# A mixture-of-experts stage on one core: large and small experts in turns, the last tiles of two experts side by side, and written orders for POOL and VectorE

## The chip, the core and the metric

One core of a Trainium2 chip runs the whole program in one launch. The metric is the device time of that launch in microseconds (us). TensorE (PE) multiplies matrices, VectorE (DVE) and ScalarE (ACT) work elementwise, GpSimd (POOL) here mainly issues indirect DMAs (gathers and scatters by a table of row numbers), and SyncE (SP) issues plain DMAs.

## The reference

A graph layer over 12500 nodes of 256 features, and behind it a mixture of 64 experts:

```
h  = feats * rsqrt(deg_out)
m  = segment_sum(h[src], dst) * rsqrt(deg_in)          # 212500 edges
x  = m @ W_gc + b_gc + feats @ W_res + b_res
vals, idx = top_k(x @ Wg + bg, 2); gates = softmax(vals)
for each expert e and each node n that chose it (at most 1024 of them):
    y[n] += gate * (gelu(x[n] @ w1[e] + b1[e]) @ w2[e] + b2[e])   # 256 -> 512 -> 256
z  = batchnorm(x + y) ;  out = layernorm(feats + z)
```

All is float32. A node has two experts, so its row of the sum is added to twice.

## The kernel before

The program has four stages one after another: degrees (to about 580 us), edge sums with the dense layer and the routing (to about 2550 us), the experts (about 2550 to 3430 us), and the two normalizations. The change touches only the experts.

Before the expert stage the kernel has x with the two gates of each node in DRAM (`x2_d`, 258 columns), the running sum in DRAM (`z_d`, which holds x), and tables that give for every expert, by slot, the row to gather and the row to add to. Experts are ranked by how many tokens they have; `TOKENS` (in units of 16) is a fixed bound for each rank, and a path for the case that it does not hold follows the stage and is skipped here. Rank i's tokens are cut into *parts* of at most four *tiles* of 128 tokens; the last tile of a rank holds what is left, 16 to 112 tokens, or is full. There are 83 parts and 241 tiles. `parts` lists them: the last rank first, then the ranks from the largest to the smallest.

For each part q the loop in the program does this:

- `begin` (L1727), called three parts ahead: on a new expert it reads the expert's number into registers of SP and VectorE (one load for up to four experts), has VectorE copy that expert's table columns (`sort_slots`), has SP load the weights (`load`, one DMA of 1026 KB and one for the bias, pool `w` with three buffers), and has POOL gather the part's rows (`gather`, L1638; pool `xg` with 16 tiles).
- `hidden` (L1667, L1671): for each of four blocks of 128 hidden units two matmuls over the part's tokens, then ScalarE's gelu into `h1`.
- `turned` (for part q + 1): VectorE computes that part's gates (`gates_of`, L1682), TensorE transposes its tiles (L1653) into the one PSUM tile `xtp`, VectorE copies it to `xT` (L1658).
- `outputs` (L1694 to L1701): for each tile four matmuls with the tokens as stationary columns and w2 as moving data into `yp` (two PSUM buffers), VectorE adds the bias (L1699) and multiplies by the gate (L1700) into `yo` (six buffers), and POOL scatters with addition into `z_d`. Scatters of one expert need not wait for each other, since no node has an expert twice; scatters of different experts do.

The order of TensorE in this stage is the program's order (`manual_schedule` for PE): hidden of q, transposes of q + 1, outputs of q. The orders of VectorE, POOL, SP and ScalarE are made by a scheduler when the program is built. [...]

## Time and profile before

| What | Value |
|---|---|
| three runs | 3574.12, 3606.88, 3612.92 us; median 3606.88 |
| the profiled execution | 3578.72 us, span 3576.8 us, mean granted TensorE clock 0.829 |
| PE busy | 2531.0 us (71%) |
| POOL busy | 2175.5 us (61%) |
| DVE busy | 1800.6 us (50%) |
| ACT busy | 798.8 us (22%) |
| expert stage, first transposes to last scatter | about 2560 to 3433 us |

The profile shows the execution on its own clock, from the first instruction of the program to the last. Shares of busy time are means over stages with different limits, so a change in one stage is read from windows inside it. Matmuls are pipelined and their ends are modelled; the difference between two starts is the better measure of what one costs. POOL's gathers and scatters appear as DMA_INDIRECT: the time is POOL's own, for issuing; the data lands later.

### The profile page before, as it was taken

What the parts mean: (1) busy time and instruction counts of PE and PEld (TensorE: products, weight loads), DVE (VectorE), ACT (ScalarE), POOL (GpSimd) and SP (SyncE); (2) the same over time, 40 slices, a digit from 0 to 9 for tenths busy, and PEclk for the clock granted to TensorE, in tenths of its full rate; (3) what the DMA queues carried; (4) which work ended last, traced back from release to release, by engine and by line L of the source; (5) the groups of instructions that cost most, each with busy time, mean ns of one, the idle gap of its engine ahead of it and who ended that gap; (6) DMA issues with size and microseconds to landing.
All of it is one profiled execution on the core that took longest, in us unless ns stands there. A gap on an engine that the chain in (4) does not pass through costs nothing. (4 is left out here: it accounts for less than half of the span.)

```text
span 3576.8 us, 40049 instructions
## 1 busy us (share of the span) xinstructions
PE 2531.0 (71%) x11797; PEld 1893.4 (53%) x11797; DVE 1800.6 (50%) x7368; ACT 798.8 (22%) x1975; POOL 2175.5 (61%) x2095
## 2 busy tenths in 40 slices
PE   2526075566776667676766666677699999999966
PEld 2415043455555555554555444454377876677856
DVE  3729454355555465655555435467543333333358
ACT  2416301122111122212221111111111221122246
POOL 7250776666666666666666666665367777777610
PEclk6657566778887878897878777788899999999988
DMA  8450853444554555555544444444555666676764
GB/s 259 128 189 6 309 203 95 158 145 144 143 150 146 141 147 168 146 147 157 155 144 122 142 117 122 119 135 124 159 115 122 134 135 146 155 177 173 197 196 144
DMA packets 313919, 538.03 MB, mean 150 GB/s; under 512 B 47274, under 2 KB 233102, under 8 KB 305502
## 3 DMA queue, kind: packets, MB, share of 16 engines
q0 software_dynamic: 119360, 266.30, 28.9%
q1 hardware_dynamic: 180795, 256.19, 23.0%
q10 hardware_dynamic: 13539, 12.90, 1.2%
q8 instruction: 97, 1.59, 0.2%
q14 instruction: 128, 1.05, 0.1%
HBM read 431.02 MB, written 105.28 MB: 150 GB/s over the span
## 5 line engine op out<-in xcount | busy, mean ns | idle before, releaser
L938 POOL DMA_INDIRECT ring<-h_d,src_col x1416 | 1372.4, 969 | 711.8 <-issue 387.2
L952 PE MATMUL p<-ring,o 128*128 128x258 f32 x2832 | 902.0, 450 | 213.2 <-issue 89.7
L952 PEld LDWEIGHTS p<-ring,o 128*128 128x128 f32 x2832 | 600.4, 224 | 389.2 <-issue 214.9
L930 DVE TENSOR_SCALAR o<-lane,rel 128x128 f32<-128x128 f32 x1416 | 356.1, 297 | 402.7 <-remote 160.3
L1701 POOL DMA_INDIRECT z_d<-yo,tables x241 | 375.0, 1556 | 129.8 <-issue 58.0
L1694 PE MATMUL yp<-w,h 128*128 128x256 f32 (+7 forms) x1928 | 436.3, 381 | 0.8 <-DVE tables L1762 0.8
L1667 PE MATMUL hp<-xT,w 128*128 128x384 f32 (+22 forms) x1328 | 392.3, 449 | 9.4 <-issue 9.4
L1694 PEld LDWEIGHTS yp<-w,h 128*128 128x128 f32 (+7 forms) x1928 | 336.8, 179 | 71.0 <-issue 7.6
L1638 POOL DMA_INDIRECT xg<-x_d,tables x241 | 234.3, 972 | 183.7 <-PE xtp L1653 88.2
L1671 ACT ACTIVATE h<-hp,w 128x384 f32<-128x384 f32 (+21 forms) x332 | 178.7, 539 | 682.0 <-PE hp L1667 673.1
L1667 PEld LDWEIGHTS hp<-xT,w 128*128 128x128 f32 x1328 | 248.0, 192 | 134.1 <-issue 61.0
L1506 ACT ACTIVATE again<-again,factor 128x256 f32<-128x256 f32 x180 | 82.4, 501 | 670.3 <-issue 363.2
L986 ACT COPY s<-p 128x258 f32<-128x258 f32 x118 | 43.8, 371 | 814.8 <-PE p L952 450.0
L1658 DVE COPY xT<-xtp 128x672 f32<-128x672 f32 (+21 forms) x83 | 70.8, 853 | 305.6 <-PE xtp L1653 297.2
L1699 DVE TENSOR_TENSOR yo<-yp,bb 128x256 f32<-128x256 f32 (+7 forms) x241 | 102.0, 423 | 224.1 <-PE yp L1694 154.2
L285 POOL DMA_INDIRECT early<-in_x,src_col x130 | 135.0, 1038 | 102.4 <-DMA early_d<-early 56.3
L567 PE MATMUL deg<-o_hi,o_lo 128*128 128x98 bf16 x1254 | 107.3, 254 | 122.8 <-issue 83.8
L1481 PE MATMUL q<-r_out,tables 128*128 128x98 f32 x360 | 66.8, 315 | 150.4 <-DVE tables L1489 55.9
L1027 PE MATMUL q<-ident,s 128*128 128x128 f32 x236 | 58.9, 337 | 158.0 <-DVE tables L1489 67.5
L222 DVE TENSOR_TENSOR o_hi<-lane_b,hi 128x2450 bf16<-128x2450 bf16 (+1 forms) x67 | 95.1, 1419 | 145.8 <-remote 106.2
L565 ACT ACTIVATE s_lo<-lane_b,nb 128x128 bf16<-128x128 bf16 x396 | 121.8, 388 | 192.9 <-remote 126.7
L567 PEld LDWEIGHTS <-o_lo 128*128 128x128 bf16 x1254 | 87.5, 125 | 140.1 <-issue 91.2
(367 smaller groups left out, 3503.5 us busy)
## 6 DMA issues: line engine op xcount, KB each, us to landing
w<-in_wpack SPq DMA_DIRECT2D x64, 1026.0 KB
again<-early_d SPq DMA_DIRECT2D x90, 256.0 KB
ring<-h_d,src_col POOLq DMA_INDIRECT x1416
early_d<-early SPq DMA_DIRECT2D x65, 256.0 KB
tables<-h_d SPq DMA_DIRECT2D x104, 128.0 KB
acc<-acc_d SPq DMA_DIRECT2D x14, 896.0 KB
acc<-in_x SPq DMA_DIRECT2D x12, 1024.0 KB
x_d<-y SPq DMA_DIRECT2D x47, 258.0 KB
```

What stands on the lines that cost most here:

```text
L285: GP.indirect_dma_start(out=t[:, c % 2], out_offset=None, in_=x, in_offset=bass.IndirectOffsetOnAxis(ap=src_col[:, MC + c : MC + c + 1], a ...
L565: S.activation(s_lo[:, i], lane_b, AF.Sign, bias=nb[:, k - k0, i : i + 1])
L567: T.matmul(deg, o_lo[:, i], o_hi[:, i], start=c + i == 0, stop=False)
L930: o_last[u] = V.tensor_scalar(o_of[u][:, j], lane, rel[:, c : c + 1], None, op0=ALU.is_equal)
L938: i = GP.indirect_dma_start(out=r[:, k, :D], out_offset=None, in_=h_d, in_offset=bass.IndirectOffsetOnAxis(ap=src_col[:, c : c + 1], axis=0),)
L952: i = T.matmul(p_of[g], o_of[v][:, n], r[:, k], start=j == 0, stop=j == GR - 1)
L1638: GP.indirect_dma_start(out=g[:r], out_offset=None, in_=x2_d, in_offset=bass.IndirectOffsetOnAxis(ap=at[:r, 0, k : k + 1], axis=0),)
L1667: T.matmul(hp[:, :m], w1[:, c, j * P : (j + 1) * P], xT[:, c, :m], start=c == 0, stop=c == 1,)
L1671: S.activation(h1[:, j, :m], hp[:, :m], AF.Gelu, bias=w[:, 2 * H + 4 * D + j : 2 * H + 4 * D + j + 1],)
L1694: T.matmul(yp[:r], h1[:, j, k * P : k * P + r], w2[:, j], start=j == 0, stop=j == 3,)
L1699: V.tensor_add(yo[:r], yp[:r], bb[:r])
L1701: st = GP.indirect_dma_start(out=z_d, out_offset=bass.IndirectOffsetOnAxis(ap=at[:r, 1, k : k + 1], axis=0), in_=yo[:r], in_offset=None, c ...
```

## The change

- **Order of the experts.** Ranks are joined into pairs (`PAIR_OF`) by how many blocks of 32 the last tile of each fills: two and two, one and three, or one and one. With the token table there are 17 pairs: five of tails of 48 or 64 tokens each, twelve of a tail of 80 or 96 beside one of 16 or 32. A pair's members follow each other, the second with its parts in reverse, so that the two tails are computed in neighbouring parts. Pairs and single ranks then alternate, the largest, the smallest, the next largest, and so on. The last rank still comes first and the one before it last. As the ranks no longer follow each other, registers are loaded for one expert at a time in most cases.
- **Tails side by side.** `pair_of_outputs` gives both tails one `yp` tile: the first at row 0, the second at row 64 or 96. For each of the four hidden blocks it issues one matmul per block of 32 columns of each tail, or one of 64 for each where both tails have 33 to 64 tokens. Each half then gets its own bias, gate and scatter. All other tiles keep `outputs` as it was, with four matmuls each (`products`).
- **Gathers of at least 80 rows** (`WHOLE`): a tail of fewer tokens gathers and transposes 80 rows; hidden, copy and output still take only its tokens.
- **Orders.** VectorE joins TensorE in the program's order. POOL's gathers and scatters are chained in the program's order (`in_order`); scatters of one expert stay free among themselves. For a pair the order on POOL is: the first tail's scatter, the gathers for three parts ahead, the second tail's scatter, the second expert's other scatters. The second's scatters wait for the first's to land.
- **Gates** (`gates`) are computed just ahead of their part's outputs, behind the copy of the next part's `xT`; before, ahead of that copy and a part earlier.
- **Buffers.** Four for the weights (three before), ten for `yo` (six before).

The diff, cut to its core:

```
-        wp = stack.enter_context(tc.tile_pool(name="w", bufs=3))
+        wp = stack.enter_context(tc.tile_pool(name="w", bufs=4))
...
-        REGS = 4
+        REGS, YO = 4, 10
...
+        def in_order(i, group=None):
+            if "over" in issued:
+                return
+            if group is None or group != issued["group"]:
+                issued.update(group=group, before=issued["these"], these=[])
+            for j in issued["before"]:
+                tc.add_manual_dep(i.ins, j.ins.name, ... NoSync, SCHED_ONLY ...)
+            issued["these"].append(i)
...
-                r = min(P, m - k)
+                r = max(WHOLE, min(P, m - k))          # WHOLE = 80
...
+        def add_to_nodes(yo, at, k, group):
...
+                for before in scatters.get(mate.get(group), []):
+                    tc.add_manual_dep(st.ins, before.ins.name, ... Sync, DATA ...)
+                scatters.setdefault(group, []).append(st)
+                in_order(st, group)
...
+        def pair_of_outputs(two_of):
+            yp = ps2.tile([P, D], F32, name="yp")
+            tails = [of[5] % P for of in two_of]
+            width = SIDE if min(tails) > BLOCK and max(tails) <= SIDE else BLOCK
+            starts = [0, max(SIDE, -(-tails[0] // BLOCK) * BLOCK)]
+            for j in range(4):
+                for start, r, (w, bb, at, gate, h1, m, group) in zip(starts, tails, two_of):
+                    for k in range(0, r, width):
+                        n = min(width, r - k)
+                        products(yp[start + k : start + k + n], n, w, h1, m - r + k, j)
+            todo = []
+            for start, r, (w, bb, at, gate, h1, m, group) in zip(starts, tails, two_of):
+                part_of_yp = slice(start, start + r)
+                yo = gated(yp[part_of_yp], r, bb[part_of_yp], gate, m // P)
+                todo.append(lambda ...: add_to_nodes(yo, at, m // P, group))
+            todo[0]()
+            return todo[1]
...
-        with tc.manual_schedule(engines={mybir.EngineType.PE}):
+        with tc.manual_schedule(engines={mybir.EngineType.PE, DVE}):
...
                 h1 = hidden(given[i][0], xT, m)
-                if q + AHEAD < len(parts):
+                if q not in pair_at and q + AHEAD < len(parts):
                     begin(q + AHEAD)
                 if q + 1 < len(parts):
                     xT = turned(q + 1)
-                outputs(*given[i], table(q), gate.pop(q), h1, m, f"expert{i}")
+                mine = (*given[i], table(q), gates(q), h1, m, f"expert{i}")
+                if q in pair_at:
+                    rest = pair_of_outputs([kept.pop(pair_at[q]), mine])
+                    begin(q + AHEAD)
+                if q in pair_at or q in pair_at.values():
+                    if q not in pair_at:
+                        kept[q] = mine
+                    mine = (*mine[:5], m // P * P, mine[6])
+                if q in pair_at:
+                    rest()
+                outputs(*mine)
```

More of the change, by code (lines that the diff above doesn't have):

```diff
@@ L110, with blocks_of @@
 ]
+SIDE, BLOCK = P // 2, P // 4
+WHOLE = SIDE + 16
+def blocks_of(r):
+    return -(-r // BLOCK)
+PAIR_OF = {}
+for _k in ((2, 2), (1, 3), (1, 1)):
+    _open = []
+    for _i, _n in enumerate(TOKENS[: E - 2]):
+        _u = blocks_of(_n * TU % P)
+        if _u not in _k or _i in PAIR_OF or _i in PAIR_OF.values():
+            continue
+        _mate = [_j for _j, _v in _open if (_v, _u) in (_k, _k[::-1])]
+        if _mate:
+            PAIR_OF[_mate[0]] = _i
+            _open = [_o for _o in _open if _o[0] != _mate[0]]
+        else:
+            _open.append((_i, _u))
 RPE = CAP // P
@@ L1629, in overfull @@
             V.tensor_copy(over_n, some)
+        issued = {"group": None, "these": [], "before": []}
+        def in_order(i, group=None):
[4 more added lines that the diff above has]
+            for j in issued["before"]:
+                tc.add_manual_dep(
+                    i.ins, j.ins.name,
+                    mybir.DependencyInfo(
+                        mybir.DependencyClass.NoSync, mybir.DependencyReason.SCHED_ONLY
+                    ),
+                    reason="gathers and scatters are issued in this order",
+                )
+            issued["these"].append(i)
         def gather(at, m):
@@ L1634, in gather @@
             for k in range(0, m, P):
-                r = min(P, m - k)
+                r = max(WHOLE, min(P, m - k))
                 k //= P
                 g = two.tile([P, D2], F32, name="xg", bufs=16)
-                GP.indirect_dma_start(
+                i = GP.indirect_dma_start(
                     out=g[:r],
@@ L1643, in gather, with turn @@
                 )
+                in_order(i)
                 xg.append(g[:r])
             return xg
-        def turn(xg):
+        def turn(xg, m):
             xtp = ps1.tile([P, 2, 4 * P], F32, name="xtp")
@@ L1655, in turn @@
                     )
-            m = k * P + r
             xT = two.tile([P, 2, 4 * P], F32, name="xT")
@@ L1686, in gates_of, with products, gated, outputs @@
             return gate
-        def outputs(w, bb, at, gate, h1, m, group):
+        def products(yp, r, w, h1, a, j):
             w2 = w[:, 2 * H : 2 * H + 4 * D].rearrange("p (c d) -> p c d", d=D)
-            for k in range(-(-m // P)):
+            T.matmul(yp, h1[:, j, a : a + r], w2[:, j], start=j == 0, stop=j == 3)
+        def gated(yp, r, bb, gate, k):
+            yo = two.tile([P, D], F32, name="yo", bufs=YO)
+            V.tensor_add(yo[:r], yp, bb)
+            V.tensor_scalar_mul(yo[:r], yo[:r], gate[:r, k : k + 1])
+            return yo[:r]
+        def add_to_nodes(yo, at, k, group):
+            r = yo.shape[0]
+            st = GP.indirect_dma_start(
+                out=z_d,
+                out_offset=bass.IndirectOffsetOnAxis(ap=at[:r, 1, k : k + 1], axis=0),
+                in_=yo,
+                in_offset=None,
+                compute_op=ALU.add,
+            )
+            if group:
+                tc.declare_no_dep(st.ins, group=group, reason="no node has an expert twice")
+                tc.add_to_no_dep_group(group, st.ins)
+                for before in scatters.get(mate.get(group), []):
+                    tc.add_manual_dep(
+                        st.ins, before.ins.name,
+                        mybir.DependencyInfo(mybir.DependencyClass.Sync, mybir.DependencyReason.DATA),
+                        reason="a node can have both experts of a pair",
+                    )
+                scatters.setdefault(group, []).append(st)
+                in_order(st, group)
+        scatters = {}
+        mate = {f"expert{j}": f"expert{i}" for i, j in PAIR_OF.items()}
+        def outputs(w, bb, at, gate, h1, m, group, ks=None):
+            for k in ks or range(-(-m // P)):
                 r = min(P, m - k * P)
@@ L1693, in outputs @@
                 for j in range(4):
-                    T.matmul(
-                        yp[:r], h1[:, j, k * P : k * P + r], w2[:, j],
-                        start=j == 0, stop=j == 3,
-                    )
-                yo = two.tile([P, D], F32, name="yo", bufs=6)
-                V.tensor_add(yo[:r], yp[:r], bb[:r])
-                V.tensor_scalar_mul(yo[:r], yo[:r], gate[:r, k : k + 1])
-                st = GP.indirect_dma_start(
-                    out=z_d,
-                    out_offset=bass.IndirectOffsetOnAxis(
-                        ap=at[:r, 1, k : k + 1], axis=0
-                    ),
-                    in_=yo[:r],
-                    in_offset=None,
-                    compute_op=ALU.add,
-                )
@@ L1710, in outputs @@
-                if group:
-                    tc.declare_no_dep(st.ins, group=group, reason="no node has an expert twice")
-                    tc.add_to_no_dep_group(group, st.ins)
+                    products(yp[:r], r, w, h1, k * P, j)
+                add_to_nodes(gated(yp[:r], r, bb[:r], gate, k), at, k, group)
+        def pair_of_outputs(two_of):
[12 more added lines that the diff above has]
+                yo = gated(yp[part_of_yp], r, bb[part_of_yp], gate, m // P)
+                todo.append(lambda yo=yo, at=at, m=m, group=group: add_to_nodes(yo, at, m // P, group))
+            todo[0]()
+            return todo[1]
@@ L1715, in gnn_moe_kernel @@
+        units = []
+        for i in range(E - 2):
+            if i not in PAIR_OF.values():
+                units.append([i, PAIR_OF[i]] if i in PAIR_OF else [i])
+        units.sort(key=lambda u: -sum(TOKENS[i] for i in u))
+        order = [E - 1]
+        while units:
+            order += units.pop(0)
+            if units:
+                order += units.pop()
+        order.append(E - 2)
         parts = []
-        for i in [E - 1, *range(E - 1)]:
+        for i in order:
             n = -(-TOKENS[i] * TU // P)
@@ L1719, in gnn_moe_kernel @@
             b = 0
+            of = []
             for j in range(k):
                 m = (n - b + k - j - 1) // (k - j)
-                parts.append((i, b, min(m * P, TOKENS[i] * TU - b * P)))
+                of.append((i, b, min(m * P, TOKENS[i] * TU - b * P)))
                 b += m
+            parts += of[::-1] if i in PAIR_OF.values() else of
+        pair_at = {}
+        for q, (i, b, m) in enumerate(parts[1:], 1):
+            if PAIR_OF.get(parts[q - 1][0]) == i:
+                assert blocks_of(m % P) + blocks_of(parts[q - 1][2] % P) <= 4
+                pair_at[q] = q - 1
         AHEAD = 3
@@ L1728, in begin @@
             i, b, m = parts[q]
-            if b == 0:
-                k = 0 if i == E - 1 else i % REGS
-                if k == 0:
-                    n = 1 if i == E - 1 else min(REGS, E - 1 - i)
+            if i not in given:
+                if i not in columns_of:
+                    n = 1
+                    at = order.index(i)
+                    while n < REGS and order[at : at + n + 1] == [*range(i, i + n + 1)]:
+                        n += 1
                     _, regs = nc.values_load_multi_w_load_instructions(
@@ L1746, in begin @@
                     )
-                    given["regs"] = regs, columns
-                regs, columns = given["regs"]
-                columns_of[i] = columns[k]
+                    for k in range(n):
+                        columns_of[i + k], reg_of[i + k] = columns[k], regs[k]
                 sort_slots(i, 0)
@@ L1752, in begin @@
                     sort_slots(i, 1)
-                given[i] = load(regs[k])
+                given[i] = load(reg_of[i])
             xg[q] = gather(table(q), m)
-        columns_of = {}
+        columns_of, reg_of = {}, {}
         def sort_slots(i, which):
@@ L1770, in turned, with gates @@
         def turned(q):
+            return turn(xg[q], parts[q][2])
+        def gates(q):
             i, b, m = parts[q]
-            gate[q] = gates_of(xg[q], snd_sorted[:, i * RPE + b : i * RPE + b + 4])
-            return turn(xg.pop(q))
-        gate = {}
+            return gates_of(xg.pop(q), snd_sorted[:, i * RPE + b : i * RPE + b + 4])
+        kept = {}
         snd_sorted = one.tile([P, NSLOT], F32)
-        with tc.manual_schedule(engines={mybir.EngineType.PE}):
+        with tc.manual_schedule(engines={mybir.EngineType.PE, DVE}):
             for q in range(AHEAD):
@@ L1794, in gnn_moe_kernel @@
                     xT = turned(q + 1)
-                outputs(*given[i], table(q), gate.pop(q), h1, m, f"expert{i}")
+                mine = (*given[i], table(q), gates(q), h1, m, f"expert{i}")
[9 more added lines that the diff above has]
+                    outputs(*mine)
+                else:
+                    outputs(*mine)
                 if q == 16:
                     overfull()
+        issued["over"] = True
         with tc.If(nc.values_load(over_n[0:1, 0:1]) > 0):
@@ L1802, in gnn_moe_kernel @@
                 r = rows(a)
-                again = two.tile([P, D], F32, name="yo", bufs=6)
+                again = two.tile([P, D], F32, name="yo", bufs=YO)
                 nc.sync.dma_start(again[:r], x2_d[a * P : a * P + r, :D])
@@ L1815, in gnn_moe_kernel @@
                     gb = gates_of(g, second[:, b : b + 4])
-                    outputs(w, bb, ab, gb, hidden(w, turn(g), 4 * P), 4 * P, None)
+                    outputs(w, bb, ab, gb, hidden(w, turn(g, 4 * P), 4 * P), 4 * P, None)
     with ExitStack() as stack:
```

## The prediction

> **What bounds the kernel now.** The change touches only the expert stage, so I read that stage first by the windows view (busy time per 100 us: PE, PEld, DVE, ACT, POOL, then the granted TensorE clock, the DMA share and GB/s).

> ```profile
> 2600.00:2700.00 100.00, 100.00 (x406) 71.58 (x405) 43.58 (x175) 19.55 (x32) 70.41 (x56) 1.00 0.56 117
> ...
> 3300.00:3400.00 100.00, 100.00 (x485) 81.67 (x484) 35.73 (x96) 22.63 (x48) 63.24 (x49) 1.00 0.77 197
> sum 800.00, PE 800.00 PEld 594.98 DVE 288.79 ACT 166.87 POOL 561.84; mean PE 100.00 PEld 74.37 DVE 36.10 ACT 20.86 POOL 70.23
> ```

> TensorE is busy 800 of 800 us at clock 1.00. Nothing that shortens only another engine's work can shorten this stretch; what counts is what TensorE itself executes, and whether something new makes it wait. The groups of the stage (from 2540 to 3440 us) say what it executes:

> ```profile
> L1694 PE MATMUL yp<-w,h 128*128 128x256 f32 (+7 forms) x1928 | 436.3, 381 | 0.8 <-DVE tables L1762 0.8
> L1667 PE MATMUL hp<-xT,w 128*128 128x384 f32 (+22 forms) x1328 | 392.3, 449 | 9.4 <-issue 9.4
> L1701 POOL DMA_INDIRECT z_d<-yo,tables x241 | 375.0, 1556 | 129.8 <-issue 58.0 <-DVE yo L1700 26.5 <-DVE gate L1682 23.8
> L1638 POOL DMA_INDIRECT xg<-x_d,tables x241 | 234.3, 972 | 183.7 <-PE xtp L1653 88.2 <-DVE tables L1762 40.8 <-issue 39.0
> L1653 PE MATMUL xtp<-ident,xg 128*128 128x128 f32 (+7 forms) x482 | 65.6, 266 | 11.0 <-issue 10.5 <-DMA xg<-x_d,tables 0.5
> ```

> 241 tiles times four blocks of the hidden size are 964 matmuls on L1694; the trace has 1928, so each float32 matmul is two passes. A busy union does not price a pass, since ends are modelled; starts do. In the timeline of PE (start, length, name, count) I subtract starts:

> ```profile
> 2660.93 5.34 PE L1694 MATMUL yp<-w,h 128*128 128x256 f32 x24
> 2666.11 5.32 PE L1667 MATMUL hp<-xT,w 128*128 128x384 f32 x16
> 2671.27 0.74 PE L1653 MATMUL xtp<-ident,xg 128*128 128x128 f32 x6
> 2671.85 5.38 PE L1694 MATMUL yp<-w,h 128*128 128x256 f32 x24
> 2677.07 1.29 PE L1667 MATMUL hp<-xT,w 128*128 128x336 f32 x4
> ```

> 24 passes of full tiles take 2666.11 - 2660.93 = 5.18 us, 0.216 each; 16 hidden passes over 384 tokens take 5.16; the transposes of two full tiles and one of 80 rows 0.58, and the outputs behind these 5.22. A tile of fewer tokens costs L1694 the same eight passes. That is what the pairing attacks: 34 of the 241 tiles.

> **The change, part by part.** *Gathers of at least 80 rows.* 24 tiles have 64 tokens or fewer, and their transposes now take 80 rows. Here are a part whose last tile has 64 tokens, then one with 16:

> ```profile
> 2713.90 0.87 PE L1653 MATMUL xtp<-ident,xg 128*128 128x128 f32 x6
> 2714.70 5.45 PE L1694 MATMUL yp<-w,h 128*128 128x256 f32 x24
> 2719.98 4.47 PE L1667 MATMUL hp<-xT,w 128*128 128x320 f32 x16
> 2724.29 0.82 PE L1653 MATMUL xtp<-ident,xg 128*128 128x128 f32 x6
> 2724.94 5.49 PE L1694 MATMUL yp<-w,h 128*128 128x256 f32 x24
> 2730.36 5.43 PE L1667 MATMUL hp<-xT,w 128*128 128x384 f32 x16
> 2735.63 0.84 PE L1653 MATMUL xtp<-ident,xg 128*128 128x128 f32 x6
> ```
> ```profile
> 2756.87 0.82 PE L1653 MATMUL xtp<-ident,xg 128*128 128x128 f32 x6
> 2757.62 5.45 PE L1694 MATMUL yp<-w,h 128*128 128x256 f32 x24
> 2762.91 3.83 PE L1667 MATMUL hp<-xT,w 128*128 128x272 f32 x16
> 2766.57 0.82 PE L1653 MATMUL xtp<-ident,xg 128*128 128x128 f32 x6
> 2767.23 5.45 PE L1694 MATMUL yp<-w,h 128*128 128x256 f32 x24
> 2772.61 5.43 PE L1667 MATMUL hp<-xT,w 128*128 128x384 f32 x16
> 2777.87 0.60 PE L1653 MATMUL xtp<-ident,xg 128*128 128x128 f32 x4
> ```

> Transposes and the outputs behind them take 0.80 + 5.28 = 6.08 us with 64 tokens and 0.75 + 5.29 = 6.04 with 16, against 0.58 + 5.22 = 5.80 with 80. So 0.24 to 0.28 us is saved per tile: 24 x 0.26 = **-6.2 us**.

> *Fewer changes to narrow outputs.* An output tile of 64 tokens or fewer lengthens its run (5.42 and 5.38 against 5.18) and the hidden passes behind it (5.27 and 5.26 against 5.16): 0.35 and 0.30 us. Before, 24 tiles pay this. After, 17 pairs and the two unpaired ones of the last two experts do: 5 x 0.32 = **-1.6 us**.

> *The pairs.* By the token table 34 tails make 17 pairs: five of two tails of 48 or 64, each one block of 64 columns; twelve of a tail of 80 or 96 beside one of 16 or 32, four blocks of 32. Before, 34 x 8 x 0.216 = 58.8 us. After, a matmul per block and hidden block: 5 x 2 x 4 + 12 x 4 x 4 = 232 matmuls, 464 passes. No row of this trace shows two blocks of columns at work, so I bound it. If no passes overlap: 464 x 0.216 = 100.2 us, +41.5. If all blocks of a pair run together, a pair takes as long as one tile: 17 x 8 x 0.216 = 29.4 us, -29.4. I take a value between, from the order in which passes stand: the two passes of a matmul follow each other on the same block of columns, so the second must wait until the first has streamed, and if later passes do not overtake it, only it and the next block's first pass can run side by side. Then n matmuls take n + 1 steps: 9 for the five pairs, 17 for the twelve, 5 x 1.94 + 12 x 3.67 = 53.8 us, **-5.0 us**. The twelve four-block pairs gain nothing in this; only the five do. In the rows above every pass starts 0.216 after the one ahead, in the order of the program, which is why I lean to the ordered value.

> [...]

> *Gates and order on VectorE and POOL.* DVE is busy 36 of 100 us, and the gates move from ahead of the transposed copy to behind it. Register loads rise from 17 to 50, each some 0.34 us, hidden behind the 64% that DVE is idle:

> ```profile
> L1740 DVEq TENSOR_LOAD <-exp_row x17: 318/343/862, 2550.6 to 2617.4; - x17
> ```

> What could hurt is the copy that feeds the next hidden matmuls, since six parts now have one full output tile (1.73 us) for cover. Before:

> ```profile
> 2876.63 0.82 PE L1653 MATMUL xtp<-ident,xg 128*128 128x128 f32 x6
> 2877.29 3.62 PE L1694 MATMUL yp<-w,h 128*128 128x256 f32 x16
> 2877.49 0.96 DVE L1658 COPY xT<-xtp 128x768 f32<-128x768 f32 x1 [2.14 <-PE xtp L1653]
> L1658 DVE COPY xT<-xtp 128x896 f32<-128x896 f32 x1 | 1.1, 1091 | 5.6 <-PE xtp L1653 5.6
> ```

> The copy starts 0.20 us after the outputs. The longest behind a one-tile part has 896 elements, 1.09 us: done at 1.29 of 1.73. Nothing is added; if the cover went, six times a few tenths.

> *POOL.* The same 241 gathers and 241 scatters, in a written order. Each has about 0.30 us of its own gap:

> ```profile
> 3253.15 1.57 POOL L1701 DMA_INDIRECT z_d<-yo,tables  x1 [0.30 <-DVE yo L1699]
> 3255.02 1.43 POOL L1701 DMA_INDIRECT z_d<-yo,tables  x1 [0.30 <-issue]
> 3257.21 1.01 POOL L1638 DMA_INDIRECT xg<-x_d,tables  x1 [0.76 <-PE xtp L1653]
> 3258.53 0.91 POOL L1638 DMA_INDIRECT xg<-x_d,tables  x1 [0.30 <-PE yp L1694]
> ```

> 241 x (0.97 + 0.30) + 241 x (1.56 + 0.30) = 754 us of a stage of some 868 (2562 to 3430): 87%, the next engine behind PE. New is a wait 17 times: the second tail's scatter waits until the first has landed. Behind it on POOL stand that expert's scatters and then the next gathers; PE waits for those only if they fall three parts behind. The last scatter of the stage gives the landing time, from the chain that ended last:

> ```profile
> 3430.93 1.53 POOL z_d L1701
> 3432.79 3.70 DMA z_d<-yo,tables
> ```

> 3.7 us from its start. The changed order puts the next part's two to four gathers between (2.5 to 5.1 us, after the first scatter's own 1.86), so the wait is covered. Were it bare, 17 x 1.8 = 31 us of the 114 that POOL has free: still no bound.

> *Order of the experts, weights in four buffers, ten output buffers.* These move loads, and PE was not waiting for any. Cost nothing while PE is at 100%. At the start of the stage PE does stand still:

> ```profile
> 2579.80 8.67 PE L1667 MATMUL hp<-xT,w 128*128 128x512 f32 x16 [8.76 <-issue]
> ```

> What ends it is not shown, so I leave it in: up to 8.8 us gained, as much lost.

> **Sum.** -6.2 - 1.6 - 5.0 = -12.8 us. On the profiled execution's own 3578.7 us (span 3576.8) that is 3565.9. That execution stands with the fastest of the other runs (3574.1, 3606.9, 3612.9; median 3606.9). I lay the change on the mean of all four, 3593.2: **3580 us**. Its own range, with the start and these runs' spread, is 3555 to 3605.

> **The rivals.** *All blocks run together.* The pairs give -29.4, in all -37.2: 3556 us (3541 on the profiled run). For it: different columns, different rows of the output. Against: the two passes on the same columns stand next to each other. It also needs POOL: 868 - 37 = 831 us against 754, or 785 with every new wait bare, so it still fits. [...]

> *No overlap at all (slower).* The place is the twelve four-block pairs: 32 passes where 16 stood, 6.9 us for 3.5. +41.5 - 7.8 = +33.7: 3627 us. It decides as soon as a four-block pair takes over 4.1 us, which eats the 7.8 us of the narrow tiles. For it: every pass in the trace is 0.216 after the other. Against: they all want the same columns there.

> *The fixed VectorE order makes PE wait.* If an output in the written order waits for its buffer, the copy behind it is late. With 0.5 us at 82 parts, +41 - 12.8: 3621 us. It decides from 0.4 us of delay at six parts and 2 us elsewhere; ten output buffers speak against it.

> **How the numbers follow.** Ordered overlap 0.38, all together 0.30, none 0.20, VectorE's order 0.12. About 1% (36 us) is what a measurement of this kernel can tell from no change. The first is within it but for the runs' spread (0.06 faster, 0.02 slower); the second, 1.03%, is beyond it 7 times in 10 (0.21); the third half the time (0.10), the last three quarters (0.09). Faster 0.27, slower 0.21, the same 0.52. The range runs from the second rival on a fast run (3537) to near the third on a slow one (3640).

> **What would show it.** On the changed L1729, a pair of two tails should take 1.9 us from start to start and a four-block pair 3.7; 1.7 in both says that all blocks overlap, 3.5 and 6.9 that none do. No transpose should have fewer than 80 rows, and the 0.24 to 0.28 should be gone. PE should stay at 100.00 in every window; idle time on L1706 released by the xT copy, or POOL above 95%, would prove me wrong, and so would a clock below 1.00.

## The result and the profile after

The changed kernel takes 3580.83 us (median of 17 runs, 3563.20 to 3605.51); beside it the kernel before took 3610.55 us (17 runs). The ratio over all runs is 0.9944, 95% interval 0.9922 to 0.9966: a gain of 0.34 to 0.78%, or 12 to 28 us. The forecast of 3580 us is met, but not by its working: the pairs brought more than five times what the sum gave them, and waits of TensorE, which the sum had at nothing, took much of the surplus back. The base helped too: the sum of -12.8 us was laid on 3593.2 us, a mean of four runs, where the median of the 17 is 3610.55 and the two medians lie 29.7 us apart. That 3580 was hit is luck.

The profiled execution after has a span of 3565.6 us against 3576.8, which is 11.2 less and close to the forecast's 12.8. That too is chance. The rows of TensorE that open and close the stage (timeline: start, length, name, count, idle before and what ended it) show it, first in the kernel before, then after:

```profile
2562.07 4.50 PE L1667 MATMUL hp<-xT,w 128*128 128x176 f32 x16 [0.66 <-issue]
...
3425.03 3.76 PE L1694 MATMUL yp<-w,h 128*128 128x256 f32 x16
```
```profile
2577.93 4.16 PE L1706 MATMUL hp<-xT,w 128*128 128x176 f32 x16 [0.62 <-DVE xT L1697]
2581.93 1.04 PE L1693 MATMUL xtp<-ident,xg 128*128 128x128 f32 x8
2582.81 3.75 PE L1729 MATMUL yp<-w,h 128*128 128x256 f32 x16
2586.49 7.13 PE L1706 MATMUL hp<-xT,w 128*128 128x512 f32 x16
...
3413.43 3.76 PE L1729 MATMUL yp<-w,h 128*128 128x256 f32 x16
```

The first hidden matmul starts at 2577.93, before at 2562.07: the unchanged stages ahead took 15.9 us more in this execution. From there to the last output run the stage takes 835.5 us, before (2562.07 to 3425.03) 863.0. So the stage gained 27.5 us. The wait of 8.76 us that stood ahead of the second part's hidden matmuls is gone: 2586.49 follows the outputs directly.

The windows that answer to those of before, the groups of the stage, and what TensorE waited for:

```profile
2600.00:2700.00 100.00, 99.37 (x487) 75.56 (x486) 37.98 (x117) 21.54 (x40) 67.17 (x53) 1.00 0.61 134
...
3100.00:3200.00 100.00, 95.93 (x477) 69.40 (x476) 38.05 (x122) 19.79 (x36) 70.72 (x57) 0.98 0.71 174
...
sum 800.00, PE 786.32 PEld 593.81 DVE 307.98 ACT 170.40 POOL 576.11; mean PE 98.29 PEld 74.23 DVE 38.50 ACT 21.30 POOL 72.01
```
```profile
L1729 PE MATMUL yp<-w,h 128*128 128x256 f32 (+5 forms) x2120 | 411.7, 383 | 8.2 <-DVE yo L1733 7.9
...
L1693 PE MATMUL xtp<-ident,xg 128*128 128x128 f32 (+3 forms) x482 | 64.8, 268 | 16.1 <-issue 10.3 <-DMA xg<-x_d,tables 5.7
```

TensorE is no longer at 100 in every window: 13.7 of these 800 us are idle, and the granted clock falls to 0.98 where it was 1.00. L1729 has 192 more passes than before (2120 against 1928: 464 in place of 272 for the pairs) and yet 24.6 us less busy time. POOL rose from 70.2 to 72.0 of 100 and is far from its limit as a mean.

What a pair takes is read from the starts. First a pair of a tail of 80 or 96 with one of 16 or 32 ahead of two full tiles (32 + 16 passes), then one of two tails of 48 or 64 ahead of one full tile (16 + 8):

```profile
2618.08 5.58 PE L1729 MATMUL yp<-w,h 128*32 128x256 f32 x48
2623.50 5.32 PE L1706 MATMUL hp<-xT,w 128*128 128x384 f32 x16
...
2711.55 3.87 PE L1729 MATMUL yp<-w,h 128*64 128x256 f32 x24
2715.26 5.32 PE L1706 MATMUL hp<-xT,w 128*128 128x384 f32 x16
```

5.42 - 16 x 0.216 = 1.96 us, and 3.71 - 8 x 0.216 = 1.98 us. The forecast said 3.7 and 1.9; both at eight steps of 0.216 (1.73) is the rival in which all blocks run together, with 0.23 and 0.25 us more. Most of that lies in two starts behind the narrow passes: in the first pair the first two passes of the full tiles start 0.33 and 0.32 us behind the one ahead, the others 0.216. The single passes in the trace say the same: in the first pair four passes start within 0.02 us, the next four 0.22 us behind them, and so on, eight times four.

### The profile page after: what moved, and what is told of

Same layout as the page of the kernel before. It is cut to its first block, busy times and chain, and to the rows that moved or that the text cites. A ratio compares the mean times of both kernels' runs of the same rounds, so it can differ in the third digit from the quotient of the medians.

```text
span 3565.6 us, 40447 instructions
## 1 busy us (share of the span) xinstructions
PE 2496.3 (70%) x11920; PEld 1876.5 (53%) x11989; DVE 1799.1 (50%) x7368; ACT 798.5 (22%) x1975; POOL 2179.6 (61%) x2095
## 4 chain that ended last, share of the span: by engine, by line
PE 38%; DVE 22%; issue 11%; another core or an unknown queue 10%; POOL 3%; DMA 3%; SPq 1%; ACT 0%; DVEq 0%; ACTq 0%; POOLq 0%
PE yp L1729 11%; PE hp L1706 10%; PE p L973 8%; DVE o L951 4%; POOL ring L959 3%; PE bank L1188 2%; PE bank L1193 2%; DVE junk L1273 1%; PE xtp L1693 1%; PE tab L1326 1%; DVE y L1211 1%; PE bank L1532 1%; DVE tables L1510 1%; DMA tables<-in_src 1%
## 5 line engine op out<-in xcount | busy, mean ns | idle before, releaser
L1729 PE MATMUL yp<-w,h 128*128 128x256 f32 (+5 forms) x2120 | 411.7, 383 | 8.2 <-DVE yo L1733 7.9
L1706 PE MATMUL hp<-xT,w 128*128 128x384 f32 (+21 forms) x1328 | 388.4, 446 | 0.8 <-DVE xT L1697 0.6
L1729 PEld LDWEIGHTS yp<-w,h 128*128 128x128 f32 (+5 forms) x2120 | 320.6, 171 | 73.1 <-issue 13.5
L1706 PEld LDWEIGHTS hp<-xT,w 128*128 128x128 f32 x1328 | 248.6, 191 | 117.4 <-issue 42.1
L1697 DVE COPY xT<-xtp 128x768 f32<-128x768 f32 (+16 forms) x83 | 70.8, 854 | 333.4 <-PE xtp L1693 300.6
L1733 DVE TENSOR_TENSOR yo<-yp,bb 128x256 f32<-128x256 f32 (+6 forms) x241 | 102.2, 424 | 174.7 <-PE yp L1729 141.3
L1502 PEld LDWEIGHTS q<-r_out,tables 128*128 128x128 f32 x360 | 62.6, 230 | 176.2 <-issue 74.4
```

The costliest lines, as they stand in the source:

```text
L1502: T.matmul(p_r[:, i], wide[:, i * P : (i + 1) * P], r_out, start=True, stop=True)
L1706: T.matmul(hp[:, :m], w1[:, c, j * P : (j + 1) * P], xT[:, c, :m], start=c == 0, stop=c == 1,)
L1729: T.matmul(yp, h1[:, j, a : a + r], w2[:, j], start=j == 0, stop=j == 3)
```

## The experiments

All runs below were made on three other chips, each against the kernel before on its own chip (medians of 3153 to 3154 us): serial, two_block, blocks_outer and ahead4 on one, after_again, before_again, free_pool and before_80 on the second, the rest on the third. The stages ahead take some 430 us less there (the first hidden matmul starts at 2144.30 us in after_again, at 2577.93 in after), so the expert stage is compared: from the start of the first hidden matmul to the start of the last output pass, read from the trace. TensorE's *own work* is the stage less its idle time in it and less what half clock costs the rest (half of each stretch in which the trace has the granted clock at 0.50). It is 853.3 us in both profiles of the kernel before, and in before_ahead4 on a third chip.

| Kernel | ratio to before, 95% | stage us | idle us | own work us |
|---|---|---|---|---|
| before, first profile | | 866.3 | 9.6 | 853.3 |
| after, first profile | 0.9944 (0.9922 to 0.9966) | 838.9 | 13.7 | 820.4 |
| before_again | one run | 863.3 | 6.1 | 853.3 |
| after_again | 0.9910 (0.9894 to 0.9927) | 838.8 | 11.8 | 819.1 |
| serial | 0.9948 (0.9931 to 0.9964) | 847.3 | 0.0 | 845.2 |
| two_block | 0.9930 (0.9914 to 0.9947) | 842.0 | 2.2 | 837.1 |
| blocks_outer | 0.9980 (0.9969 to 0.9991) | 855.4 | 0.0 | 852.4 |
| ahead4 | 0.9872 (0.9855 to 0.9888) | 819.1 | 0.0 | 816.2 |
| free_pool | 0.9915 (0.9899 to 0.9932) | 833.5 | 9.7 | 819.1 |
| gathers_first | 0.9940 (0.9924 to 0.9957) | 853.3 | 19.8 | 820.8 |
| ahead4_dve_free | 1.0037 (1.0024 to 1.0050) | 871.2 | 38.8 | 823.3 |
| ahead4_narrow | one run | 824.1 | 0.0 | 822.0 |
| before_80 | one run | 859.6 | 6.8 | 847.2 |
| before_ahead4 | 0.9999 (0.9990 to 1.0009) | 860.0 | 5.0 | 853.3 |

Stage, idle time and own work are those of one profiled execution; the ratios go over all runs. The expectations count idle time a little more widely, with the short waits just ahead of the first hidden matmul (up to 2.7 us more), and the first of them count the stage from the first transposes, 2.3 us earlier (841 us).

The theory behind the first four runs: blocks of columns run fully side by side, and the rest of the gain is lost to gathers that come late. The rival is the forecast's own, ordered overlap.

**serial.** Each tail of a pair as a tile of its own:

```
-            yp = ps2.tile(...)          # one tile for both tails, a matmul per block
+            for r, (w, ...) in zip(tails, two_of):
+                yp = ps2.tile(...)
+                for j in range(4):
+                    products(yp[:r], r, w, h1, m - r, j)
```

> The changed kernel with one thing undone: the two tails of each of the 17 pairs are computed one after the other, as a tile of its own each (34 tiles of 8 passes), in the same order of experts and with the same written orders. Theory A (all blocks of a pair run together, 1.73 us of passes a pair): the outputs cost 17 x 8 x 0.216 = 29.4 us more, and the stage from the first transposes to the last output, 841 us in the changed kernel, is 29 us longer less whatever waits of TensorE the pairs had brought (up to some 15 us): 855 to 870 us. Theory B (the forecast's ordered overlap, pairs worth 5.0 us): 5 to 7 us longer, 846 to 848. If TensorE's waits behind the pairs come from the four-column-block passes themselves, the late completions of output tiles vanish here; if they come from the written orders of POOL and VectorE, they stay.

Measured: 847.3 us with nothing idle. That is only 8.5 us above the changed kernel, less than theory A's lowest, and near theory B's 5 to 7: taken alone it would have favoured the wrong one. What decides is the idle time, which went with the pairs; beside ahead4, which also waits for nothing, the pairs are worth 845.2 - 816.2 = 29.0 us of TensorE's own work. (The medians of the whole runs, 3137.05 and 3114.26 us, lie 22.8 apart; the other stages differ by some us from one execution to the next.)

**two_block.** The same for the twelve pairs with blocks of 32 alone (`if not (min(tails) > BLOCK and max(tails) <= SIDE)`: one tail after the other).

> The changed kernel with only the five pairs of two 64-column blocks side by side; the twelve pairs with blocks of 32 columns are computed one tail after the other. Theory A (full overlap): 12 x 8 x 0.216 = 20.7 us more in the outputs, less the waits that the four-block pairs bring. Theory B (ordered overlap): the four-block pairs had gained nothing, so no difference beyond 1 us. If the four-block passes are what delays completions, TensorE is back at 100 per cent here apart from waits for gathers; if the orders are, its idle time stays near 20 us.

Measured: 842.0 us, 2.2 idle. TensorE's own work, 837.1, stands between serial's 845.2 and ahead4's 816.2: the five two-block pairs give 8.1 us, the twelve four-block pairs 20.9. Theory A's 20.7 is met; B had the twelve at nothing.

**blocks_outer.** The order of the loops in a pair turned round:

```
-            for j in range(4):
-                for start, r, (...) in zip(...):
-                    for k in range(0, r, width):
+            for start, r, (...) in zip(...):
+                for k in range(0, r, width):
+                    for j in range(4):
```

> The changed kernel with the passes of a pair in another program order: all four hidden blocks (8 passes) of one block of columns, then the next block of columns, in place of one matmul for each block of columns in turn. If each block of columns runs its own queue whatever the order, a four-block pair still takes 1.97 us from start to start and the stage is unchanged at 841 us. If passes only start in program order, and a pass waits for the one ahead on its own columns, a four-block pair takes 32 - 3 = 29 steps of 0.216, 6.3 us, and a two-block pair 15 steps, 3.2 us: 12 x 4.3 + 5 x 1.3 = 58 us more.

The two pairs shown above, in this kernel (timeline of TensorE):

```profile
2183.26 8.25 PE L1729 MATMUL yp<-w,h 128*32 128x256 f32 x48
2191.35 5.32 PE L1706 MATMUL hp<-xT,w 128*128 128x384 f32 x16
...
2281.17 4.79 PE L1729 MATMUL yp<-w,h 128*64 128x256 f32 x24
2285.79 5.32 PE L1706 MATMUL hp<-xT,w 128*128 128x384 f32 x16
```

8.09 - 3.46 = 4.63 us and 4.62 - 1.73 = 2.89, in place of 1.96 and 1.98: neither expectation. Less the 0.3 us that is left over, these are 20 and 12 steps of 0.216. With 32 passes in four runs of eight, 20 = 32 - 3 x 4; with two runs, 12 = 16 - 4: the last four passes of a block run beside the first four of the next. The single passes show just that: four start alone, then three times four steps have two starts each, 0.005 to 0.06 us apart (in the two-block pair once), and the last four start alone again. So order does count; why the distance is four passes was not shown. The stage is even longer than serial's (855.4 against 847.3 us). In the changed kernel's order two passes for each block follow each other, and four start together (1.96 us).

**ahead4.** `AHEAD = 4`, and 20 buffers for gathered tiles.

> The changed kernel with parts begun four ahead in place of three, and 20 buffers for gathered tiles in place of 16. Theory A (TensorE's waits for gathers come from POOL being late by a few us where several small tails follow each other): the 5.7 us of waits for gathered rows go, and with them some us at half clock behind them; stage 841 to about 830 us. Rival (POOL is behind for good there, its gathers stand behind scatters in the written order, and an earlier place changes nothing, or a fifth part's weights wait for a buffer): 841 us within 3, or longer.

Measured: 819.1 us with nothing idle, shorter than expected. The windows of both (sums and means over 2150 to 2950 us), the changed kernel's second profile first, and what TensorE waited for in it and here (the 0.6 and the 0.4 are waits just ahead of the stage):

```profile
2550.00:2650.00 100.00, 94.51 (x446) 70.71 (x445) 36.12 (x113) 19.96 (x37) 74.07 (x60) 0.97 0.64 144
...
sum 800.00, PE 788.22 PEld 595.80 DVE 309.60 ACT 170.74 POOL 574.79; mean PE 98.53 PEld 74.48 DVE 38.70 ACT 21.34 POOL 71.85
```
```profile
2550.00:2650.00 100.00, 100.00 (x482) 74.91 (x481) 40.52 (x127) 21.19 (x38) 75.03 (x60) 1.00 0.73 169
...
sum 800.00, PE 800.00 PEld 605.71 DVE 316.47 ACT 175.78 POOL 584.93; mean PE 100.00 PEld 75.71 DVE 39.56 ACT 21.97 POOL 73.12
```
```profile
PE xtp L1693 <- DMA xg<-x_d,tables: 12.4, 12, 2.9
...
PE hp L1706 <- DVE xT L1697: 0.6, 1, 0.6
```
```profile
PE hp L1706 <- DVE xT L1697: 0.6, 1, 0.6
PE xtp L1693 <- DMA xg<-x_d,tables: 0.4, 1, 0.4
```

TensorE is back at 100.00 at clock 1.00. This is the version that beats both kernels: 1.28% below before, against 0.90% for the changed kernel, each on its own chip. That difference is some 12 us, give or take 8 by the two intervals; the 838.8 - 819.1 = 19.7 us between the stages are those of two single executions.

**after_again, before_again.** Both kernels unchanged, profiled once more.

> The changed kernel itself, profiled a second time. Its first profile had the stage (first hidden matmul to last output pass) at 838.9 us with TensorE idle 14.8 us in it, while the same kernel with parts begun four ahead has 819.1 us with 1.1 us idle. Theory A (gathers three parts ahead come too late where small tails follow each other, so the waits belong to the kernel): 832 to 842 us again, idle 10 to 15 us, at the same parts. Rival (that one execution was disturbed): 819 to 824 us, idle under 4 us, and then four ahead brings nothing.

> The kernel before, profiled a second time. Its first profile had 866.3 us from the first hidden matmul to the last output pass, with one wait of 8.8 us at the second part. If that wait belongs to the kernel (the second part's gathers and tables are always late), 862 to 868 us again; if it was an accident of that execution, 855 to 858 us, and then 9 us of the changed kernel's shorter stage are not its own.

Measured: 838.8 us and 11.8 idle, 863.3 us and 6.1 idle. The changed kernel's waits are its own. Here all of them are for gathered rows (the rows above); the first profile put 7.9 us down to VectorE's L1733 instead, at pairs. The places agree only in part (waits stand about 217, 230, 447 and 788 us behind the first hidden matmul in both). At the longest of the first profile VectorE had itself stood idle, though the pair's passes had started by 3104.8:

```profile
3108.82 0.42 DVE L1733 TENSOR_TENSOR yo<-yp,bb 96x256 f32<-96x256 f32 x1 [4.58 <-remote]
```

What held it there was not settled.

The wait at the start of the kernel before is its own too, 5.5 us the second time.

One of the waits, in the second profile (timeline of TensorE, then of POOL, then of SyncE, of the same stretch):

```profile
2609.61 3.62 PE L1706 MATMUL hp<-xT,w 128*128 128x256 f32 x16
2613.07 0.82 PE L1693 MATMUL xtp<-ident,xg 128*128 128x128 f32 x6
2616.82 0.44 PE L1693 MATMUL xtp<-ident,xg 128*128 128x128 f32 x2 [2.93 <-DMA xg<-x_d,tables]
```
```profile
2580.38 1.38 POOL L1739 DMA_INDIRECT z_d<-yo,tables  x1 [4.97 <-DVE yo L1733]
...
2587.68 1.01 POOL L1677 DMA_INDIRECT xg<-x_d,tables  x1 [0.30 <-issue]
...
2599.75 1.64 POOL L1739 DMA_INDIRECT z_d<-yo,tables  x1 [0.86 <-issue]
...
2609.31 0.95 POOL L1677 DMA_INDIRECT xg<-x_d,tables  x1 [0.30 <-issue]
2610.57 1.63 POOL L1739 DMA_INDIRECT z_d<-yo,tables  x1 [0.30 <-DVE yo L1733]
...
2616.86 0.94 POOL L1677 DMA_INDIRECT xg<-x_d,tables  x1 [0.30 <-issue]
```
```profile
2609.91 0.33 SPq L1635 DMA_DIRECT2D w<-in_wpack  x1
```

The gather that ends the wait was issued at 2609.31 and landed at 2616.78 by its semaphore, 0.04 us ahead of the transpose. From 2587.68 to 2617.80 POOL has no gap but its own 0.30 and one of 0.86: with a mean of 72% it is at its limit for these 30 us. A tile costs it 3.13 us (the prediction's 0.97 + 0.30 and 1.56 + 0.30), and few tokens save little: in the kernel before, with tiles of 16 to 128 rows, all gathers take it 0.86 to 1.11 us and all scatters 1.31 to 1.74. TensorE does not outrun that: in ahead4, where it waits for nothing, no three to eight neighbouring parts take it less than 3.15 us a tile (before_again: 3.33). But POOL has hardly any room left to catch up. It had stood idle for 4.97 us at 2580.38, until VectorE had the next rows to scatter, and 5.80, 6.83 and 5.10 us (up to 2354.53, 2501.6 and 2540.91) ahead of all other late gathers but the last. That these pauses made it late is read from the trace and not tested.

The landing is the other half. This gather took 7.5 us to land, and a weight load of 1026 KB was issued 0.6 us behind it. Three of the eleven waits in the stage end with such a gather (6.5 to 7.5 us to land, a weight load under way) and make up 6.2 of the 11.8 us. The gathers behind the other eight waits landed in 2.7 to 3.4 us and were issued too late: 5.6 us. The change has put many more gathers beside a weight load: from 1 us ahead of a load's issue to 4 us behind it stand 20 of the 241 gathers in before_again and 84 in after_again. Those land after 5.3 and 6.5 us in the median, the others after 2.8 and 2.9. In ahead4 it is 85, but the longer lead hides them. No run takes the loads and the gathers apart.

**free_pool.** `in_order` returns at once, so POOL's order is the scheduler's.

> The changed kernel without the written order on POOL: gathers and scatters stand where the scheduler puts them; the pair's second tail still waits for the first tail's scatter to land. Theory A1 (the written order holds gathers behind scatters that wait for the landing or for VectorE): TensorE's waits go, stage 819 to 825 us. Theory A2 (POOL is at its limit between small tails whatever the order, and three parts ahead are too few): 832 to 845 us.

Measured: 833.5 us, 9.7 idle; the ratio is the changed kernel's (0.9915 against 0.9910). Theory A2: the written order did not make the gathers late.

**gathers_first.** `begin(q + AHEAD)` ahead of a pair's outputs, as at all other parts.

> The changed kernel, three parts ahead, with the gathers of a pair's second part begun ahead of the pair's outputs as at every other part; on POOL they stand ahead of the first tail's scatter and no longer between the two scatters. If the gathers are late because they stand behind that scatter, TensorE's 12 to 13 us idle fall below 6 and the stage to 825 to 832 us, though the second scatter's wait for the landing is then bare (up to 17 x 3 us on POOL). If three parts are too few wherever the gathers stand, or the bare wait costs as much, 835 to 845 us.

Measured: 853.3 us and 19.8 idle in the profiled execution, worse than either expectation. That execution is the slowest of five, 12 us above their median. By the ratios, 0.9940 (0.9924 to 0.9957) against 0.9910 (0.9894 to 0.9927), some 9 us are lost, so the usual stage is nearer to 848 (an estimate from these ratios).

```profile
PE xtp L1693 <- DMA xg<-x_d,tables: 20.6, 21, 2.6
```

The gathers stand earlier and yet are later as a whole. The second tail's scatter now waits bare for the first's landing and holds all that follows: POOL waits 18.2 us in the stage for scatters to land, up to 5.6 at a time, against 8.6 and up to 2.0 in after_again. That this alone makes the gathers late is not shown. The place between the two scatters was the better one.

**ahead4_dve_free.** `manual_schedule(engines={PE})` in ahead4: VectorE's order left to the scheduler.

> The changed kernel begun four ahead, with VectorE's order left to the scheduler as before (TensorE's and POOL's stay written). If the wait at the second part of the kernel before (8.8 and 5.5 us idle in its two profiles, none in any kernel with VectorE's order written) came from VectorE's scheduled order, with table copies and gates of later parts ahead of the first outputs, it is back: stage 825 to 832 us. If POOL's scheduled order had made it (gathers for many parts ahead of the first scatters), it stays away here: 818 to 821 us.

Measured: 871.2 us, 38.8 idle, far outside. What TensorE waited for:

```profile
PE hp L1706 <- DVE xT L1697: 25.9, 14, 3.5
PE yp L1729 <- DVE yo L1733: 14.8, 14, 2.5
```

The expectation looked at the start alone. There the idle time comes back in part (2.0 us just ahead of the stage, 0.8 and 0.6 in it); the other 37 us are spread over the stage. VectorE's written order is worth 52 us here, by the stage and by the ratios, and is a condition of the whole change.

**ahead4_narrow, before_80.** Gathers of only a tail's rows in ahead4 (`r = min(P, m - k)`), and of at least 80 in the kernel before.

> The changed kernel begun four ahead (stage 819.1 us, TensorE at 100 per cent), with gathers and transposes of only the rows a tail has, down to 16. The prediction's term for the narrow transposes, 24 x 0.26 = 6.2 us, should come back whole, since nothing hides it: 825.3 us. Rival, from the kernel before with 80 rows alone (TensorE's own time 4.9 us less): 824 us. A third: with pairs the outputs behind the transposes start narrow anyway, and only the few narrow transposes ahead of full tiles cost: under 3 us.

> The kernel before with one part of the change alone: gathers of at least 80 rows, so that no transpose is narrower than 80. The prediction's term is 24 tiles x 0.26 = 6.2 us less in the stage, and the transposes of a last tile of 16 rows and the outputs behind them at 5.80 us in place of 6.04. Rival: the narrow transposes' price is paid by the narrow outputs right behind them anyway, and less than 2 us goes.

Measured: 824.1 us, 5.0 above ahead4; and 859.6 with 6.8 idle. In TensorE's own work that is 822.0 - 816.2 = 5.8 us and 853.3 - 847.2 = 6.1 us (the 4.9 in the expectation leaves half clock in). The term was 6.2.

**before_ahead4.** The kernel before with `AHEAD = 4`, 20 buffers for gathered tiles and four for weights.

> The kernel before with parts begun four ahead, 20 buffers for gathered tiles and four for weights, and nothing else of the change. If what four ahead repairs was made by the pairs and the new order of experts (TensorE waits for nothing in the kernel before once the stage runs), the stage stays at 860 to 868 us and the ratio at 0.998 to 1.002. Rival: four ahead shortens any of these kernels by some 20 us, and the changed kernel's own gain is smaller than it looks: 840 to 848 us.

Measured: 860.0 us, ratio 0.9999. Four ahead repairs only what the change made.

## Why the prediction was right, and where it was wrong

TensorE's own work is 853.3 us before, 819.1 in after_again and 816.2 with four ahead. The first rival's sum, -37.2 us, was right for ahead4 (-37.1); its 3556 us was not reached. The forecast's number came true, its mechanism did not: what it had wrong worked in opposite directions, and the low base did the rest. By the prediction's steps:

- *Narrow transposes, -6.2:* right, 5.8 and 6.1 measured. No transpose has fewer than 80 rows any more.
- *Fewer narrow outputs, -1.6:* about right. serial has no tails side by side, and its own work is 853.3 - 845.2 = 8.1 us less than that of the kernel before; less the transposes, about 2 us are left. Stretches of narrow output passes fall from 24 to 19 in the traces. No run has this alone.
- *The pairs, -5.0:* **this step failed.** The working let only neighbours in program order overlap, n + 1 steps for n matmuls. Measured are eight steps for either kind of pair, 29.0 us in all against the bound of 29.4. The row it leaned on, full tiles starting 0.216 apart in order, says nothing on blocks: those passes all want the same columns. No run shows the 3.67 us of the working, in which a matmul's second pass waits for its first and no pass starts ahead of an earlier one; 1.96 speaks against it. In blocks_outer order does show (4.63 us for the same 32 passes, four of each block started ahead of the next block's first).
- *POOL, nothing:* **failed as well.** 754 us of work in 831 was a mean over the stage. POOL stands idle for 5 to 7 us at a time ahead of scatters, and at 3.13 us a tile beside TensorE's 3.15 to 3.4 it is slow to catch up. The prediction did name the condition ("PE waits for those only if they fall three parts behind") and did not look at any stretch.
- *Order of the experts and weights in four buffers, cost nothing:* **failed.** The loads that these move stand beside four times as many gathers as before (84 against 20), which land 3.6 us later than the others. Together with POOL's lateness the price is 838.8 - 819.1 = 19.7 us in the profiled executions: 11.8 of idle time, 5.0 of half clock behind it, and 2.9 not accounted for. By the ratios of all runs it is about 12.
- *The wait for the landing, covered by the gathers:* right in the main. Even so POOL waits for landings 10 times in the first profile, 18.5 us, and 6 times in the second, 8.6. In gathers_first, where the wait is bare, it is 18.2, with the longest of all (5.6).
- *VectorE's order, nothing, or a rival that makes PE wait:* the rival was wrong way round. In this order of experts it is the scheduler's order that makes TensorE wait. The register loads on VectorE rose to 61 in the trace, and not to 50, without harm.
- *The start, up to 8.8 either way:* the wait went in every kernel with VectorE's order written, 6 to 10 us of idle time.
- *Clock 1.00, PE at 100.00:* wrong, as the windows show. After the longest wait of the first profile eight passes take 3.4 us where 1.73 are usual:

```profile
3110.23 3.58 PE L1729 MATMUL yp<-w,h 128*128 128x256 f32 x8 [3.48 <-DVE yo L1733]
3113.65 4.68 PE L1706 MATMUL hp<-xT,w 128*128 128x336 f32 x16
```

So the -24.5 us in the stage (863.3 to 838.8) are: -29.0 pairs, -8.1 transposes and narrow outputs, -6.1 idle time and -1.0 half clock at the start, and +19.7 given back. The terms are read from executions on two chips. The forecast's 12.8 was an underestimate on both sides.

## What to carry to other kernels

Try tails of few output rows side by side: here, in float32, two of them took 1.96 to 1.98 us, where one full tile takes 1.73, with the blocks of columns given in turn. With each block's passes in one run, the pairs cost more than tails computed one after the other (855.4 against 847.3 us). Once the busiest engine gets faster, look for the next one stretch by stretch and not by its mean: a POOL at 72% was late in bursts, and gathers near a weight load's issue landed later (6.5 us against 2.9 in the median of after_again). Both held TensorE up for 20 us in the profiled execution, and one more part of lead took them back. Before a written order is called neutral, try the same kernel without it.
